# A fused four-layer network: where the windowed attention's first projections and its late score stacks stand in the order of work

## The chip, the cores and the metric

The kernel runs on one NeuronCore of one Trainium2 chip, as one program. The core has five engines with an instruction queue each, and they meet only through semaphores: TensorE (PE, matmuls from SBUF into the eight banks of PSUM, with its weight loads shown apart as PEld), VectorE (DVE), ScalarE (ACT, which works functions such as Exp and Gelu from tables that it has to load), GpSimd (POOL) and SyncE (SP, which here issues most DMA transfers). The metric is the time of one execution on the device in microseconds; less is better.

## What is computed

The input x holds 8 sequences of 256 tokens with 128 features each. Twelve sub-layers are added to it in turn: half a feed-forward layer, a mixer, half a feed-forward layer, in each of four macaron layers, every one of them behind a layer normalisation without parameters. The changed code is in the third macaron layer:

```python
x = x + 0.5 * _L2_ffn_ref(_layernorm(x, axis=-1), ...)      # 16 experts, top 4
x = x + _L2_attn_ref(_layernorm(x, axis=-1), ...)           # linear and windowed attention
x = x + 0.5 * _L2_ffn_ref(_layernorm(x, axis=-1), ...)      # the same 16 experts again

def _L2_attn_ref(x, ...):
    h = _layernorm(x, ln_g, ln_b)
    lin_out = _linear_attention(h @ wq_lin + bq_lin, h @ wk_lin + bk_lin, h @ wv_lin + bv_lin)
    win_out = _window_attention(h @ wq_loc + bq_loc, h @ wk_loc + bk_loc, h @ wv_loc + bv_loc, rel_bias)
    gate_in = jnp.concatenate([lin_out, win_out, h], axis=-1)
    gate = jax.nn.sigmoid(jnp.maximum(gate_in @ wg1 + bg1, 0.0) @ wg2 + bg2)
    out = gate * lin_out + (1.0 - gate) * win_out
    return out @ wo + bo + x
```

The linear attention takes elu(q) + 1 and elu(k) + 1, sums k times v over a sequence and divides by a sum of q times k. The windowed attention has 16 heads of 8 features; each token looks at the 65 tokens within 32 of it, with a learned bias for each distance, and a softmax. The experts compute gelu(x w1 + b1) w2 + b2 with 128 features and 256 hidden units for all 16 experts, weighted by the routing (zero for twelve of the sixteen). The layers before are a sign-weighted feed-forward layer, full softmax attention, a top-2 expert layer and four Mamba layers; those behind are a low-rank quantised feed-forward layer and another attention.

## The kernel before

**Stages.** The stream x stays in SBUF for the whole program, transposed, as xT (128 features by 2048 tokens). `tile_macaron` runs a list of stages: Attn0, Moe1, Mamba, Moe1, Moe2, Attn2, Moe2, Attn3. Expert stages work on four chunks of 512 tokens (CH), attention stages on eight sequences of 256 (SEQ). A stage has `open` (its pools, loads, constants), `steps` or `prepare` (a generator of what must be done before a chunk or sequence can be worked on: normalisation, projections), `main` (the work itself, also a generator), `enter` (what is made once the stage before has ended) and `run`. A stage's pools lie on the other side of SBUF from those of the stage before.

**The wished order.** Everything is issued by generators that are woven together. `weave` (L314) steps through the main generator and, after its step i, draws steps of the generator `ahead` as long as `at * MAIN < i * prep`, where `at` counts the steps drawn. `joined` and `early` take two generators in turns, the second for n steps at most; `mix` shares turns by size. So class constants say what is prepared beside what: MAIN is the number of main's steps, PREP the number of steps of the next stage's generator to be drawn beside the last chunk of the stage before, and EARLY two numbers of steps to be drawn beside the second and the third chunk. Where they are not set, EARLY is (0, 0). `Moe.run` (L530) opens the next stage at its second chunk and passes it those steps at the second, third and fourth chunk. `Attn2.run` uses Attn2's PREP too, in its own loop over sequences: beside the main work of sequence s it draws the steps of `mix(stack(s + 1), project(s + 2))`, which has 29 of them.

**The real order.** The Tile framework then schedules these instructions again with a simulated timeline, so the order of each engine's queue is not the source's; a build's listing of each engine's instructions tells it.

**The experts (Moe2).** `main` works each of 16 experts in two halves of 128 hidden units: matmuls into a bank `h`, the Gelu on ScalarE (32 a chunk, 128 in all), a multiplication by the routing weight on VectorE, a split into a rounded high part `yh` (ScalarE) and the rest `yl` (GpSimd), and matmuls into the bank `o`. The routing weights come as `c<-rows` transfers that SP issues; three such tiles are kept in turn. At a chunk's end VectorE adds `o` to xT.

**Attn2, for each sequence.** The diff touches this class.

- `project` (L1821): the two normalisations (ln_c is the centred tile, pp a bank for a projection, `rsqrt` takes a power on GpSimd), h; then q and k of the windowed attention, each as a rounded part `hi` and the rest `lo`, written to DRAM (`scr`, three writes for each); then the linear attention: `em` (an exponential), `ql`, `kv`, `ek` (an exponential), `kvs`, `den`, `lin`. Ten steps.
- `stack` (L1903): brings `scr` back into the stacked tiles of one of three sets; four heads share the 128 partitions, 32 for each, of which 24 hold hi, hi and lo, and two more hold the row maxima on the side of q and ones on the side of k. Then the row maxima: in two halves (the first and the second maxima), eight times a matmul of qs and ks with a matmul that adds the band of biases, into a bank `mx`, and a maximum on VectorE (`nm`, L1946). A transposition brings the 16 maxima of a half into rows, ScalarE and VectorE round them into `nh` and `nl`, and SP issues four transfers that put them into qs (L1957), so that the scores come out of the matmuls with the maximum already subtracted. 19 steps.
- `main` (L2011): eight tiles of scores (`sp`), VectorE adds the band (`pr`), ScalarE takes the exponential in place, and matmuls by vs and by ones sum into the bank `acc`; then the division, the gate and the output projection (`tail`). MAIN is 11, its number of steps.

**The sets.** `stacks` (L1782) makes a set: qs (128 x 4 x 256), ks (128 x 4 x 4 x 256), vs. Each ks[:, e] holds the keys of one head in four and must be zero in the partitions of the others, so the whole set is filled with zeros first and later only partly written. The fills are copies of a broadcast zero: qs on VectorE (L1791), ks for e = 0 and 2 on VectorE (L1797) and for e = 1 and 3 on ScalarE (through `m.act`, whose instructions all have line L175), each of 128 x 1024; four DMAs write the ones (L1798), and GpSimd clears vs (L1802). Sequences use the sets in the order 0, 1, 2, 0, 1, 2, 1, 0 (SETS). Set 0 is made in `open`, at the experts' second chunk. Sets 1 and 2 are made in `enter`, behind the experts' last chunk, in the pool "a2s", since they lie where the experts' tiles were. Set 0 is given up only with the whole stage. In the trace the experts' matmuls, bias additions and so on have the line of the helper that issued them: L142 for matmuls, L151 for `tt`, L175 for `act`, L171 for the loading of a table in front of an activation, L209 for yl.

Of the kernel before, what the change touches and what calls it, by code (L numbers as in the profile page):

```python
# [255 lines left out]
class Stage:  # L256
# [3 lines left out]
    EARLY = (0, 0)  # L260
# [27 lines left out]
    def enter(self):  # L288
        pass
# [109 lines left out]
class Moe(Stage):  # L399
# [130 lines left out]
    def run(self, st, then):  # L530
        ready, after = list(st), None
        for c in range(NCH):
            if c == NCH - 3:
                with self.m.behind():
                    after, gen = then()
                splits, left = after and after.splits(), after and len(after.todo)
            st = ready.pop(0)
            if c == NCH - 1:
                n = after.PREP if after else 0
                if left:  # L540
                    gen, n = self.early(gen, splits, left), n + left
                return self.weave(self.main(c, st), (after, gen), n)
            to, rest, n = c + self.DEPTH, self.m.rest, 0
            own = self.steps(to) if to < NCH else iter(())
            parts = [rest] if rest else []
            if c >= NCH - 3 and left:

                parts.append((splits, len(after.todo) // 3))
                left -= len(after.todo) // 3
            if c >= NCH - 3 and after:  # L550

                parts.append((gen, after.EARLY[c - NCH + 3]))
            for part in parts:
                own, k = self.joined(own, *part)
                n += k
            st = self.weave(self.main(c, st), (self, own), (self.PREP if to < NCH else 0) + n)
            if to < NCH:
                ready.append(st)
            if rest:
                self.m.rest = self.m.under.close()  # L560


class Moe1(Moe):


    MAIN, PREP, EARLY = 9, 7, (1, 8)
# [85 lines left out]
class Moe2(Moe):  # L652


    MAIN, PREP, EARLY = 16, 16, (1, 3)
# [218 lines left out]
class Attn0(Stage):  # L874


    MAIN, PREP = 17, 12
# [315 lines left out]
class Mamba(Stage):  # L1193


    MAIN, PREP, EARLY = 16, 44, (2, 16)
# [539 lines left out]
class Attn2(Stage):  # L1736


    MAIN, PREP = 11, 30

    SETS = (0, 1, 2, 0, 1, 2, 1, 0)

# [39 lines left out]
    def stacks(self, pool, i):  # L1782

        nc = self.nc
        qs = self.t(pool, [P, 4, SEQ], f"qs{i}", dtype=F32R)
        ks = self.t(pool, [P, 4, 4, SEQ], f"ks{i}", dtype=F32R)
        vs = self.t(pool, [P, 2, 4, 160], f"vs{i}")
        none = self.one[:, 8:9].to_broadcast([P, 4 * SEQ])  # L1790
        nc.vector.tensor_copy(qs[:].rearrange("p m t -> p (m t)"), none)  # L1791
        for e in range(4):
            dst = ks[:, e].rearrange("p m t -> p (m t)")
            if e % 2:
                self.m.act(dst, none, AF.Copy)
            else:
                nc.vector.tensor_copy(dst, none)  # L1797
            nc.sync.dma_start(  # L1798
                ks[32 * e + 24 : 32 * e + 26, e].bitcast(F32),
                self.ones[:].unsqueeze(1).to_broadcast([2, 4, SEQ]),  # L1800
            )
        nc.gpsimd.memset(vs[:], 0.0)  # L1802
        return qs, ks, vs
# [173 lines left out]
    def enter(self):  # L1977
        self.ps = self.pool("a2p", 2, late=True, space=PSUM)
        self.mk = self.pool("a2m", 2, late=True)
        self.more = ExitStack()  # L1980
        tp = self.m.tc.tile_pool(name="a2s", bufs=1, side=self.side, reuse_waits="tile")
        sk = self.more.enter_context(tp)
        self.sets += [self.stacks(sk, 1), self.stacks(sk, 2)]

    def run(self, st, then):
        ready, half = st
        for s in range(NB - 2):
            ahead = self, self.mix(self.stack(s + 1, half), self.project(s + 2))
            ready, half = self.weave(self.main(s, ready), ahead)
        after, gen = then(False)  # L1990
        n = after.EARLY[1] if after else 0
        main = self.main(NB - 2, ready)
        st = self.weave(main, (self, self.early(self.stack(NB - 1, half), gen, n)), 19 + n)
        self.more.close()
        rest = []

        def main():
            rest.append((yield from self.main(NB - 1, st)))

        if after:  # L2000
            after.load()
        res = self.weave(main(), (after, gen), after and after.PIECES)
        if after is None:
            self.finish(rest[0])
        else:

            m = self.m
            m.rest, m.under, self.sb = (rest[0], 4), self.sb, ExitStack()
        return res
# [84 lines left out]
class Attn3(Stage):  # L2094


    MAIN, PREP, EARLY = 5, 10, (4, 9)
# [130 lines left out]
    def project(self, s):  # L2228
# [54 lines left out]
        with m.tc.issue_after(moved.ins):  # L2283
            for i, st in enumerate(stacks):
                for e in range(2):

                    for n, k in enumerate((0, 0, 1) if i else (1, 0, 0)):
                        at = 64 * e + 16 * n
                        nc.sync.dma_start(
                            st[at : at + 16, :, :].rearrange("d (h b) t -> d h (b t)", b=2).bitcast(F32),  # L2290
                            scrs[i][k].rearrange("(h e d) t -> e d h t", e=2, d=16)[e],
                        )
        yield
        return *stacks, vs, hs

    def values(self, hs):
# [301 lines left out]
```

## Time and profile before

The time is 2558.17 us, the median of three executions (2551.15 to 2559.72). The profile was taken of one more execution:

| | us |
|---|---|
| the profiled execution | 2557.26 |
| its span, first to last instruction | 2555.5 |
| PE busy, 11655 matmuls | 2302.1 (90%) |
| VectorE busy | 1938.1 (76%) |
| ScalarE busy | 1879.4 (74%) |
| GpSimd busy | 1608.0 (63%) |
| PE's mean granted clock | 0.954 of full speed |
| bytes moved by DMA | 271.65 MB, 106 GB/s |

The stages around the change, from the windows of the trace (busy us of each engine, and PE's granted clock):

| stage | from to | length | PE | VectorE | ScalarE | GpSimd | clock |
|---|---|---|---|---|---|---|---|
| Moe2, first | 1490 to 1742 | 252 | 239.1 | 198.0 | 200.1 | 151.3 | 0.99 |
| Attn2 | 1742 to 1957 | 215 | 189.2 | 167.4 | 111.8 | 30.8 | 0.97 |
| Moe2, second | 1957 to 2200 | 243 | 226.0 | 178.9 | 187.1 | 126.6 | 0.98 |

The limits of the stages are those that the trace of xT's updates shows, to about a microsecond, and work of neighbouring stages overlaps there. A row of windows gives, behind the limits, the length, then for each of PE, weight loads, VectorE, ScalarE and GpSimd the busy us with the number of instructions in brackets, then PE's granted clock, the DMA engines' busy share and GB/s. A row of the chain of waits has the start, the length and the engine with tile and line; "x2" stands for two instructions running on, "issue" for time in which the engine waited for nothing that the profile shows.

### The profile page before, as it was taken

Reading aid. Unit: us, or ns where it says so; the run is one execution under the profiler, and the core shown is the slowest. Engines: PE = TensorE matmul, PEld = TensorE weight load, DVE = VectorE, ACT = ScalarE, POOL = GpSimd, SP = SyncE. Lnnn points to the kernel's source line nnn. Section 1 sums busy time; section 2 is a strip of 40 time slices with the busy share of each in tenths; the row PEclk is TensorE's granted clock in tenths of the full one; section 3 lists DMA queues with packets and bytes.
Section 4 is the critical chain, followed back from the end, with each engine's and each line's share of the span. In section 5 each row is a group of like instructions: output and inputs, shape, how many; then the busy total and the mean of one; then the engine's idle time right before and its main releaser. Section 6 shows DMA issues by size and latency. Waiting matters only on the chain. (4 is left out here: it accounts for less than half of the span.)

```text
span 2555.5 us, 36909 instructions
## 1 busy us (share of the span) xinstructions
PE 2302.1 (90%) x11655; PEld 1429.0 (56%) x11655; DVE 1938.1 (76%) x3150; ACT 1879.4 (74%) x4373; POOL 1608.0 (63%) x1194
## 2 busy tenths in 40 slices
PE   6999999988988898988897899998998999799997
PEld 5776776843333333333322577776776777566665
DVE  3655666558999999999999788867877877477664
ACT  5877877797777777777764578785555788799885
POOL 2657555559899999999988676552112555554432
PEclk8999999999899999999988899999999999999998
DMA  6676656233444433344432593321225324234420
GB/s 163 173 191 187 159 122 178 75 93 75 104 102 104 111 78 82 84 120 101 93 75 58 151 285 121 110 87 46 71 56 180 114 75 116 41 64 70 79 46 9
DMA packets 138275, 271.65 MB, mean 106 GB/s; under 512 B 19328, under 2 KB 43456, under 8 KB 137696
## 3 DMA queue, kind: packets, MB, share of 16 engines
q1 hardware_dynamic: 136576, 265.56, 40.6%
q10 hardware_dynamic: 1248, 3.48, 0.6%
q8 instruction: 93, 1.52, 0.3%
q14 instruction: 102, 0.84, 0.1%
q0 software_dynamic: 256, 0.25, 0.0%
HBM read 151.54 MB, written 33.16 MB: 72 GB/s over the span
## 5 line engine op out<-in xcount | busy, mean ns | idle before, releaser
L1528 POOL TENSOR_TENSOR hs<-hs,cl 128x1024 f32<-128x1024 f32 x256 | 602.3, 2371 | 68.0 <-DVE hs L1522 43.3
L1522 DVE TENSOR_TENSOR_SCAN hs<-dA,up 128x1024 f32<-128x1024 f32 x192 | 439.1, 2287 | 23.8 <-DVE up L151 0.9
L142 PE MATMUL y<-hs,ysel 128*64 128x512 f32 x1024 | 305.6, 679 | 30.6 <-POOL hs L1528 26.8
L1162 POOL TENSOR_SCALAR pr<-pr,sums 128x256 f32<-128x256 f32 x192 | 175.9, 925 | 166.1 <-DVE sums L1157 149.8
L175 ACT ACTIVATE dA<-dt,negA 128x510 f32<-128x510 f32 x384 | 252.0, 715 | 0.2
L151 DVE TENSOR_TENSOR up<-up,du 128x1024 f32<-128x1024 f32 x192 | 233.3, 1215 | 20.4 <-PE up L142 14.9
L175 ACT ACTIVATE h<-h,vec 128x512 f32<-128x512 f32 x256 | 168.4, 667 | 54.1 <-PE h L142 50.9
L142 PE MATMUL pp<-xp,w 128*128 128x512 f32 x480 | 173.7, 482 | 26.9 <-ACT pre L175 26.2
L235 POOL TENSOR_TENSOR ln_r<-ln_r,mhalf 128x2 f32<-128x2 f32 (+2 forms) x116 | 90.4, 781 | 168.5 <-ACT ln_r L175 166.3
L142 PEld LDWEIGHTS pp<-xp,w 128*128 128x128 f32 x480 | 90.3, 201 | 126.8 <-ACT pre L175 61.7
L1482 POOL TENSOR_TENSOR hs<-du,bl 128x1024 f32<-128x1024 f32 x64 | 151.6, 2369 | 1.8 <-DVE pre L151 1.8
L1522 DVE TENSOR_TENSOR_SCAN hs<-up,hs 128x1024 f32<-128x1024 f32 x64 | 145.0, 2265 | 0.2 <-ACT up L175 0.2
L209 POOL TENSOR_TENSOR yl<-y,yh 128x512 fp32r<-128x512 f32 x64 | 83.0, 1297 | 96.7 <-ACT yh L175 93.2
L175 ACT ACTIVATE pr<-sp,nmax 128x256 f32<-128x256 f32 x256 | 121.7, 487 | 26.1 <-DVE nmax L1149 7.1
L142 PE MATMUL up<-bp,bsel 128*128 128x512 f32 x192 | 101.6, 530 | 41.6 <-DVE hs L1522 38.6
L142 PEld LDWEIGHTS y<-hs,ysel 128*64 128x64 f32 x1024 | 54.1, 144 | 144.3 <-issue 76.5
L175 ACT ACTIVATE ln_q<-pp 128x128 f32<-128x128 f32 x348 | 98.9, 284 | 38.0 <-PE pp L142 33.7
L209 POOL TENSOR_TENSOR yl<-z,yh 128x512 fp32r<-128x512 f32 x72 | 92.2, 1292 | 51.6 <-ACT yh L175 44.0
L1149 DVE TENSOR_REDUCE nmax<-sp 128x2 f32<-128x512 f32 x128 | 87.5, 687 | 48.7 <-PE sp L142 47.8
L151 DVE TENSOR_TENSOR h<-h,c 128x512 f32<-128x512 f32 x128 | 89.1, 696 | 36.9 <-ACT h L175 29.5
L142 PE MATMUL h<-hh,wh 128*128 128x512 f32 x256 | 104.9, 410 | 9.5 <-DVE y L151 7.5
L175 ACT ACTIVATE ln_c<-pp,ln_r 128x128 f32<-128x128 f32 x332 | 99.5, 375 | 16.7 <-POOL ln_r L235 16.0
(444 smaller groups left out, 6836.6 us busy)
## 6 DMA issues: line engine op xcount, KB each, us to landing
c<-rows SPq DMA_DIRECT2D x64, 512.0 KB
cl<-states SPq DMA_DIRECT2D x62, 512.0 KB
c<-rows SPq DMA_DIRECT2D x64, 256.0 KB
dt<-dt SPq DMA_DIRECT2D x128, 128.0 KB
du<-du SPq DMA_DIRECT2D x128, 128.0 KB
k<-kh SPq DMA_DIRECT2D x60, 256.0 KB
kl<-kl SPq DMA_DIRECT2D x60, 256.0 KB
st<-scr SPq DMA_DIRECT2D x96, 128.0 KB
```

Of the source, the lines that this page charges most:

```text
L142: return self.pin(self.nc.tensor.matmul(out, lhsT, rhs, start=start, stop=stop))
L151: return self.pin(self.nc.vector.tensor_tensor(out, in0, in1, op))
L175: i = self.nc.scalar.activation(out, in_, func, **kw)
L209: i = (lower or self.nc.vector).tensor_tensor(lo, x, hi, ALU.subtract)
L235: self.nc.gpsimd.tensor_tensor(out, out, self.mhalf[:, 0 : out.shape[-1]], ALU.pow)
L1149: nc.vector.tensor_reduce(nmax[:], sp[:], AX.X, ALU.max, negate=True)
L1162: self.turned = nc.gpsimd.tensor_scalar(pr[:, t, :], pr[:, t, :], sums[:, t : t + 1], None, ALU.mult)
L1482: self.m.pin(self.nc.gpsimd.tensor_tensor(self.hs[g][:], du[:], b, ALU.mult))
L1522: m.pin(nc.vector.tensor_tensor_scan(x[:].rearrange("p g t -> p (g t)"), self.decays.pop(g).rearrange("p g b t -> p (g b t)"), u[:].rearra ...
L1528: m.pin(nc.gpsimd.tensor_tensor(x[:], x[:], c, ALU.mult))
```

## The change

Three things, all in Attn2.

1. The steps of its generator that are drawn beside the experts: none at the second chunk, 10 at the third and 20 at the fourth, in place of none, none and 30. As PREP is used in the stage's own loop too, there 20 of 29 steps are wished beside the main work of a sequence, and the other nine behind it.
2. The four ks fills of sets 1 and 2 all go to ScalarE, in place of two of each set. Set 0's stay shared between VectorE and ScalarE.
3. `enter` makes only set 1; `run` makes set 2 behind the main work of sequence 0 (in the source), before the steps of sequence 2, the first that uses it, are drawn.

```diff
 class Attn2(Stage):
-    MAIN, PREP = 11, 30
+    MAIN, PREP, EARLY = 11, 20, (0, 10)
...
         for e in range(4):
             dst = ks[:, e].rearrange("p m t -> p (m t)")
-            if e % 2:
+            if e % 2 or i:
                 self.m.act(dst, none, AF.Copy)
             else:
                 nc.vector.tensor_copy(dst, none)
...
         tp = self.m.tc.tile_pool(name="a2s", bufs=1, side=self.side, reuse_waits="tile")
-        sk = self.more.enter_context(tp)
-        self.sets += [self.stacks(sk, 1), self.stacks(sk, 2)]
+        self.sk = self.more.enter_context(tp)
+        self.sets.append(self.stacks(self.sk, 1))

     def run(self, st, then):
         ready, half = st
         for s in range(NB - 2):
             ahead = self, self.mix(self.stack(s + 1, half), self.project(s + 2))
             ready, half = self.weave(self.main(s, ready), ahead)
+            if s == 0:
+                self.sets.append(self.stacks(self.sk, 2))
```

## The prediction

> **What bounds the kernel now.** I read the busy table by slices first, to see which engine is full around the edited stage, then PE's busy time by windows, then the chain of waits across the hand-over, then single engines in order of time. The edit touches 1587 to 1833 us: the first 16-expert stage's last three chunks, and the first two sequences of the linear and window attention behind it. The x updates of VectorE at 1586.9, 1639.1, 1686.0 and 1741.9 us end the experts' four chunks. The third and fourth, by windows (length, then busy us and instructions of PE, weight loads, VectorE, ScalarE, GpSimd, then PE's granted clock, DMA):
>
> ```profile
> 1639.10:1686.00 46.90, 46.77 (x203) 38.03 (x204) 34.22 (x56) 34.99 (x61) 25.64 (x25) 1.00 0.37 115
> 1686.00:1741.90 55.90, 52.25 (x234) 39.79 (x233) 38.29 (x78) 47.70 (x84) 28.92 (x34) 1.00 0.19 62
> ```
>
> PE is full in the third chunk and loses 3.6 us in the fourth, nearly all of it where ScalarE changes its function table. Then the hand-over, by the same columns:
>
> ```profile
> 1741.70:1748.30 6.60, 1.91 (x9) 1.18 (x8) 6.36 (x10) 3.90 (x4) 2.81 (x2) 0.89 0.03 7
> 1748.30:1752.00 3.70, 3.60 (x13) 3.12 (x14) 2.76 (x6) 0.00 (x0) 0.00 (x0) 0.50 0.05 11
> 1752.00:1757.30 5.30, 2.81 (x11) 1.73 (x9) 1.49 (x7) 2.50 (x11) 1.40 (x2) 0.82 0.17 50
> 1757.30:1761.60 4.30, 4.25 (x17) 3.62 (x17) 1.84 (x4) 2.31 (x5) 0.00 (x0) 0.63 0.54 138
> ```
>
> PE stands idle for 7.3 us of these 20 and runs much of the rest at half its clock. The chain of waits (start, us, what) says why:
>
> ```profile
> 1742.63 0.81 DVE qs L1791
> 1743.44 2.25 DVE ks L1797 x2
> 1745.69 0.40 DVE nm L1946
> 1746.09 0.60 DVE qs L1791
> 1746.69 1.20 DVE ks L1797 x2
> 1747.89 0.41 DVE nm L1946
> ...
> 1748.35 1.98 PE pp L142 x6
> ...
> 1754.85 0.44 SPq L1957
> 1755.28 0.04 issue
> 1755.33 1.78 DMA qs<-nl
> 1757.11 0.25 issue
> 1757.35 1.19 PE sp L142 x4
> ```
>
> VectorE's six fills of sets 1 and 2 stand between the row maxima (nm) of sequence 0, which hold PE's three free banks; these fills cost 4.86 us of the path. Only when the last maxima have gone by DMA into qs may the scores (sp) start, 15.4 us behind the experts' last matmul.
>
> **EARLY and PREP: sequence 0 sooner.** Ten steps of the generator are drawn in the third chunk and 20 in the fourth instead of 30 in the fourth, so as before some ten are left to the hand-over in the source. The scheduler reorders them, so I go by the order listing of both builds, counting the experts' 128 Gelus. Sequence 0's em exponential moves from behind Gelu 102 to 74, its ek from 104 to 78, its lin from 110 to 84; sequence 1's hi from 118 to 93, its em from 118 to 112, ek from 122 to 118. Its normalisation, hi, lo and scr writes were in the third chunk already. Five of the eight second maxima, both matmuls of sequence 1's centring and the transposition of the maxima now stand ahead of the experts' last two matmuls: eight pairs of a set and band matmul at 0.30 us from start to start, 2.4, centring, transposition and two ln_c 0.6, so 3.0 us of PE work goes in front of the experts' end. As PE is full there, that end moves back 3.0 us; it is moved, not added.
>
> ScalarE pays in the third chunk. Its 35.0 us of 46.9 get two exponentials (0.42), four table loads (1.28 each), three copies (1.0) and sequence 1's normalisation, h and hi (4.8): 11.8 together, so 46.8, just as much as PE has. The rows for one exponential:
>
> ```profile
> 1686.23 1.28 ACT L171 ACT_TABLE_LOAD   x1
> 1687.52 0.42 ACT L175 ACTIVATE em<-em 128x256 f32<-128x256 f32 x1
> 1687.96 1.28 ACT L171 ACT_TABLE_LOAD   x1
> ```
>
> Each excursion withholds 3.0 us from the Gelus. PE has four h banks to ride it out: the two of sequence 0 cost PE 1.3 us of idle now, the two of sequence 1 (held open for 8.4 us) 1.9. Least: all four as cheap as the first two, 2.5 us. Most: fully exposed, 12. With the third chunk's ScalarE full but the fourth's down to 36 of about 53 us, I take 4.4 against 3.9 us now (0.5 worse; ends -1.4 and +8).
>
> The row shows the load ending 0.01 us before the exponential. The Trainium skill, page "ScalarE: Activation LUTs", section "What ACT_TABLE_LOAD costs", adds a 1.38 us drain to the same 1.28 us load and so speaks against this move; no drain stands in these rows. By it the four loads of the third chunk would take 10.6 us instead of 5.1, which would put ScalarE 5.5 us over.
>
> SP issues the same 14 scr transfers (0.36 to 0.6 us each) ahead of other c<-rows loads. Of those three are kept in turn, and SP waits for their buffers, not they for SP (28.4 us for six issues behind 1656.8); cost nothing under that cover, 0.4 to 0.9 us a transfer without. On GpSimd one of sequence 1's powers (0.71) now stands before the last yl (1.28): up to 0.7 at the experts' end, inside the 4.4. PREP also paces the attention's own six sequences (20 of their 29 steps instead of all): I cost this at nothing, because the listing has the same PE order in both builds from sequence 1's second maxima to the last sequence. Without that, nine steps with the 4.7 us from maxima to scores would come bare six times, 28 us.
>
> **Fills: four from VectorE to ScalarE, set 2 later in the source.** No fill may start before the experts' last matmul (ScalarE's now start at 1741.70, released by PE o). VectorE loses four (3.45 us on the chain) and keeps two qs (0.81 and 0.60), which now stand behind all the maxima. ScalarE has eight instead of four. The row:
>
> ```profile
> 1741.70 3.90 ACT L175 ACTIVATE ks<-one 128x1024 fp32r<-128x1024 f32 x4 [1.68 <-PE o L142]
> ```
>
> In the listing both sets' fills stand before the first pr exponential, so "a sequence later" is not what the queue does. From the experts' last matmul, T': set 1 until 3.9, two ln_c 0.6, set 2 until 8.4, first exponential 0.7, first acc at T' + 9.2. Behind those fills wait all pr exponentials and, through them, all acc matmuls. GpSimd's two memsets (2.81) run beside it.
>
> PE in the meantime: from the transposition of the maxima to the first scores took 5.4 us (1751.91 to 1757.35: nh, nl, four issues on SP, 1.78 us of DMA). The transposition now stands about 1.4 us before T', so scores start at T' + 4.0; five tiles of them, paced by VectorE's 0.80 a tile, and 0.9 us of others end near T' + 8.5. Then set 1's own DMAs: behind the maxima's issues (T' + 1.8) SP has eight of ones and zeros at 0.7, eight of scr at 0.41, then 3.0 us to landing (as at 1885.01): set 1's first maxima at T' + 13.2.
>
> **The sum.** Before, set 1's first maxima start 18.9 us behind the experts' end with 6.2 us of matmuls at full clock between: 12.7 lost (7.3 idle, the rest half clock). After, 13.2 with 6.2 (five tiles of scores and two of acc in place of the maxima): 7.0 lost, 5.7 better. Then set 1's second maxima wait for nl by DMA with 1.9 us of other matmuls to cover it instead of 5.1: 3.8 lost to 2.3, 1.5 worse. 5.7 - 1.5 - 0.5 = 3.7 us. The profiled span of 2555.5 lies in a run of 2557.26, 0.9 below the median of 2558.17: I expect 2554.4. With the exponentials' loss at its least, 2.5 us, it is 2552.5, with all 12 us of it 2562. The second experts and the last attention are shuffled a little in the listing; 43 us of PE idle lie there in 555, and I allow 3 either way. Three runs lay 8.6 us apart.
>
> As to the clock, the row has 0.50 from 1748.3 to 1752 behind 4.8 us of idle in 6.6. The Trainium skill ("TensorE: Matmul & The Clock Gate", "Part 1: The HAM clock gate") says that one idle window of about 3.4 us halves the clock until as long a busy one. By that the 4.0 us hole left at T' would be followed by scores at half rate, 3 us of them costing 1.5 more; as they end before ScalarE does, the sum would stay.
>
> **Rivals.**
> ScalarE becomes the bound of the third chunk (slower, 0.24): for it, 46.8 us against 46.8 and a queue kept in order; against, PE lost only 1.3 us at two excursions. It decides once more than 8.1 us of the 12 are exposed; at 12, 2562.
> The hole closes further (faster, 0.20): ScalarE waits on nothing in the fourth chunk and all table loads cost 2.5, and the second maxima's DMA stays covered (1.5): 2554.4 - 1.9 - 1.5 = 2551; with the late shuffle at its good end 2548. For it: 12.7 us are lost there; against, eight fills in a row.
> The change does not do what it says (0.08): the reordering scheduler had half of sequence 0's projections in the third chunk already; gain and loss cancel, 2558.
> My forecast has 0.48.
>
> **The numbers.** About 0.3%, 7.7 us, is what a measurement here can tell from no change: faster is below 2550.5, slower above 2565.8. Faster: half of the second rival and 0.12 of the forecast's lower tail, 0.22. Slower: 0.10 of the first, 0.06 for what the late shuffle may add, 0.16. The range: 2554.4 less 5 and the shuffle's 3, 2546; 2562 and 2 of the 3, 2564. The forecast's own is 2550 to 2559.
>
> **What would show it.** Right: ScalarE near 47 us in the third chunk; eight ks fills back to back, ending 8.4 us behind the experts' last matmul with pr right behind; first maxima on set 1 near 13 us behind it; no L1797 on VectorE but set 0's; the loop at 26 us a sequence as before. Wrong: PE idle before h matmuls at the exponentials of the third chunk beyond 4 us, a loop longer than that, or a hand-over as long as 19 us.

## The result, and the profile after

The changed kernel takes 2563.61 us (median of 10 executions, 2559.82 to 2570.26) against 2558.11 us of the kernel before (10 executions, 2551.15 to 2566.96): a ratio of 1.0028, with an interval of 1.0014 to 1.0041. A second comparison, 12 executions against 35, gave 1.0004 (0.9987 to 1.0021). So the change costs between nothing and some 7 us where 3.7 us of gain were forecast; the time lies in the stated range (2546 to 2564), but on the other side of the time before from the forecast. The profiled execution took 2564.42 us, with a span of 2562.6.

The third and fourth chunk of the experts, by windows (length, then busy us and instructions of PE, weight loads, VectorE, ScalarE, GpSimd, then PE's granted clock, DMA share, GB/s):

```profile
1642.40:1698.40 56.00, 54.25 (x249) 43.88 (x248) 41.63 (x76) 45.32 (x82) 28.96 (x31) 1.00 0.35 111
1698.40:1752.30 53.90, 49.00 (x209) 37.34 (x207) 37.59 (x67) 39.41 (x70) 26.18 (x28) 0.97 0.15 50
```

The third chunk has grown from 46.9 to 56.0 us, the fourth has shrunk from 55.9 to 53.9. ScalarE is busy for 45.3 of the third's 56.0 us and is not its bound. PE does more there (249 matmuls instead of 203) and is idle for 1.75 us instead of 0.1, in the fourth for 4.9 instead of 3.65. Then ScalarE's queue in order of time (start, length, line, what):

```profile
1752.11 3.89 ACT L175 ACTIVATE ks<-one 128x1024 fp32r<-128x1024 f32 x4
1755.91 0.60 ACT L175 ACTIVATE ln_c<-pp,rs 128x128 f32<-128x128 f32 x2
1756.41 3.89 ACT L175 ACTIVATE ks<-one 128x1024 fp32r<-128x1024 f32 x4
1760.20 1.36 ACT L175 ACTIVATE pr<-pr 128x640 f32<-128x640 f32 x2
```

That is the queue as it was forecast: both sets, one behind the other, and the first score exponential 8.1 us behind the start of the fills (forecast 8.4). The chain of waits across the hand-over (start, us, what):

```profile
1751.58 0.51 PE o L142
1752.09 0.02 issue
1752.11 1.11 ACT ks L175 x2
...
1754.02 1.99 ACT ks L175 x2
1756.01 0.51 ACT ln_c L175 x2
1756.51 0.96 ACT ks L175
1757.47 0.29 SPq L1798
...
1760.54 0.42 SPq L1916
...
1762.26 3.16 DMA ks<-scr
1765.41 0.83 issue
1766.25 1.03 PE mx L142 x4
```

No VectorE fill stands on it any more. Fills, SP's issues and the transfer of the keys follow each other, and set 1's first maxima (mx) start 13.9 us behind the end of the experts' last matmul (1752.31), forecast 13.2, before 18.9.

So where did the loss come from? The x updates of VectorE cut the span into stages that the kernels share. The table counts from the start of the last x update of the Moe1 stage (1530.18 us in the profile of before), to which the expectations below refer as the first chunk's end; "x of sequence 1" is the update that ends the edited attention for sequence 1. (Moe2 begins there, not at 1490 us as the table of stages had it.) Two profiles stand for each of three programs; the fills alone are the third and tenth run below.

| us from there to | before | changed | fills alone |
|---|---|---|---|
| the experts' end | 211.8, 211.9 | 219.4, 219.7 | 211.8, 212.0 |
| x of sequence 1 | 291.6, 293.1 | 292.4, 294.3 | 290.6, 292.2 |
| x of sequence 3 | 344.3, 344.8 | 344.1, 346.0 | 342.3, 343.9 |
| the second experts' end | 658.4, 663.1 | 659.2, 662.2 | 655.4, 657.7 |
| the end | 1022.7, 1025.3 | 1026.5, 1031.2 | 1014.1, 1015.6 |
| length of the last attention | 364.3, 362.2 | 367.2, 369.0 | 358.7, 358.0 |

By means, the changed kernel is 0.5 us late at sequence 3, on time (-0.1) at the end of the second experts, and 4.9 late at the end of the program. The edited stage came out even, and the loss lies in the last attention (with the feed-forward layers woven into it), some 440 us behind the edit. No line of it was touched: the scheduler put its instructions in another order. (Between two profiles of one program this table differs by up to 4.7 us, so its single rows are rough; the experiments below say how far the order can be told from chance.)

### The profile page after: what moved, and what is told of

It is laid out like the page before. It is cut to its first block, busy times and chain, and to the rows that moved or that the text cites. A ratio compares the mean times of both kernels' runs of the same rounds, so it can differ in the third digit from the quotient of the medians.

```text
span 2562.6 us, 36926 instructions
## 1 busy us (share of the span) xinstructions
PE 2313.9 (90%) x11655; PEld 1437.7 (56%) x11655; DVE 1936.6 (76%) x3146; ACT 1883.3 (73%) x4377; POOL 1607.4 (63%) x1194
## 5 line engine op out<-in xcount | busy, mean ns | idle before, releaser
L142 PE MATMUL up<-bp,bsel 128*128 128x512 f32 x192 | 100.8, 526 | 37.8 <-DVE hs L1522 35.3
L142 PE MATMUL h<-hh,wh 128*128 128x512 f32 x256 | 104.5, 408 | 11.4 <-DVE y L151 7.7
```

The lines of the kernel that those rows point to most:

```text
L142: return self.pin(self.nc.tensor.matmul(out, lhsT, rhs, start=start, stop=stop))
```

## The experiments

The profiles compare stages, the ratios whole runs. Each variant is built from the kernel before (b) or the changed one (a). The listing tells which order PE has in the last attention: B is that of the kernel before, A that of the changed one, F that of the third run, L that of the fourth. These letters are not those of the theories A to D in the expectations. The traces show the same four orders: within one letter all 2,055 matmuls behind the second experts stand in one order (run 2 departs from B by 14).

**One part at a time.** Runs 1 and 2: the early steps alone, and with set 2 made later.

```diff
 b, run 1
-    MAIN, PREP = 11, 30
+    MAIN, PREP, EARLY = 11, 20, (0, 10)
 run 2: the same, and set 2 made behind s == 0 as in the change
```

> The kernel before with the first part alone: MAIN, PREP, EARLY = 11, 20, (0, 10). PE's order in the last attention is that of the kernel before, word for word. Theory A (the edited region gains about what it loses, and the 5.5 us of the whole change lie in the new order of the last attention): 2558 +- 3, region from the first chunk's end to the x update of sequence 2 at 318.6 +- 2 us as before. Theory B (the steps drawn early stall PE beside the experts, and that is the loss): 2561 to 2564, with the third and fourth chunk some 7 us longer and at most 4 us won back behind them. Theory C (the fills in a row on ScalarE are the loss): 2553 to 2556, since here VectorE's six fills no longer stand between the second maxima.

> The first and the third part: steps drawn early, set 2 made a sequence later, its fills and set 1's shared between VectorE and ScalarE as before. PE's order behind the second sequence is that of the kernel before but for some 30 rows. Theory A: 2555 to 2559. Theory B: 2561 to 2564, like the first run. Theory C: 2550 to 2555, as neither engine has more than three fills of a set in a row.

Ratios 1.0003 (0.9984 to 1.0021) and 1.0004 (0.9987 to 1.0021), with medians of 2564.60 and 2561.27 us where the kernel before took 2560.79 in the same comparison. The experts' end is at 219.4 and 217.8, 7.6 and 6.0 us late, and given back by sequence 3 (342.9 and 343.6). The last attention takes 361.8 and 364.7 us, with order B. Theory C, which expected a gain of the first run, is out. The experts' end is late as theory B says, but nothing of it is left at sequence 3, where theory B had at most 4 us won back.

Runs 3 and 4: the fills alone, and the fills with set 2 later.

```diff
 b, run 3
-            if e % 2:
+            if e % 2 or i:
 run 4: the same, and set 2 made behind s == 0 as in the change
```

> The second part alone: all eight ks fills of sets 1 and 2 on ScalarE, steps drawn as before. The last attention's order differs from both kernels' in some 1000 rows. Theory A: the hand-over gains about 3.4 us (four fills of 0.6 to 1.1 us leave VectorE's queue between the maxima), and the total is anything from 2552 to 2562, by the order of the last attention alone. Theory B: 2554 to 2556. Theory C: the first score exponential waits for eight fills; hand-over as long as before or longer, 2560 to 2564.

> The second and third part: the change without the steps drawn early. Theory A: hand-over 3 us shorter, total 2552 to 2562 by the last attention's order. Theory B: 2553 to 2556, the gain of the fills without the experts' stalls. Theory C: 2560 to 2564.

Ratios 0.9974 (0.9956 to 0.9991) and 0.9998 (0.9982 to 1.0014). With the fills alone the kernel is faster: 2553.77 us against 2560.79. At sequence 3 both are 2.0 us ahead of the first profile of before (342.3, 342.2; but the third run's kernel came to 343.9 in its second profile), and the last attention takes 358.7 us with order F and 365.3 with order L. Theory C expected the third run to be slower than before, and theory B 2553 to 2556 us of the fourth, which took 2560.73.

**The same region with another end.** The listing of a build tells its order before it runs, and small edits around the hand-over leave the last attention in one of a few orders. So regions and ends can be paired. Run 5 is the changed kernel again; the others:

```diff
 a, run 6: set 2's qs fill on GpSimd                          (end B)
-        nc.vector.tensor_copy(qs[:].rearrange("p m t -> p (m t)"), none)
+        (nc.gpsimd if i == 2 else nc.vector).tensor_copy(qs[:].rearrange("p m t -> p (m t)"), none)
 a, run 7                                                     (end F)
-    MAIN, PREP, EARLY = 11, 20, (0, 10)
+    MAIN, PREP, EARLY = 11, 20, (0, 9)
 run 3's kernel, run 8                                        (end A)
-    MAIN, PREP = 11, 30
+    MAIN, PREP, EARLY = 11, 29, (0, 1)
```

> The changed kernel once more, beside its variants. Theory A (the order that the scheduler gives the second experts and the last attention is the loss): ratio 1.002 to 1.003, from the first chunk's end of the first experts to the x update of sequence 3 within 1 us of before, the last attention 366 to 368 us against 362 to 364 of the kernel before and of the first run, which have one order there. Theory D (the edited stage is the loss, the last attention is noise): ratio the same, the last attention 362 to 365.

> The changed kernel, with set 2's qs fill on GpSimd instead of VectorE. PE's order around the hand-over differs from the changed kernel's in 78 rows; in the last attention it is word for word that of the kernel before. Theory A: the loss is gone, ratio 0.999 to 1.001, the last attention 362 to 365 us. Theory D: as the changed kernel, 1.002 to 1.003.

> The changed kernel with EARLY (0, 9) instead of (0, 10). Around the hand-over its order is close to the changed kernel's; in the last attention it is word for word that of the third run (the fills alone), which was the fastest there, 358.7 us. Theory A: ratio 0.997 to 0.999, the last attention 358 to 360. Theory D: 1.001 to 1.003.

> All eight fills on ScalarE, both sets at the hand-over, one step drawn in the third chunk and 29 in the fourth. The hand-over is near the third run's; behind it, from the third sequence to the end, the order is the changed kernel's but for 7 rows, in the last attention word for word. Theory A: the last attention 366 to 368 us and the ratio 1.000 to 1.003, though the hand-over gains as in the third run. Theory D: 0.996 to 0.998 like the third run.

| run | end | x of sequence 3 | last attention | ratio |
|---|---|---|---|---|
| 5, changed again | A | 346.0 | 369.0 | 1.0004 (0.9987 to 1.0021) |
| 6 | B | 351.0 | 362.2 | 1.0006 (0.9990 to 1.0022) |
| 7 | F | 346.0 | 356.9 | 0.9980 (0.9965 to 0.9996) |
| 8 | A | 344.5 | 364.9 | 1.0000 (0.9985 to 1.0015) |

Run 5's ratio misses what both theories expected (1.002 to 1.003), and its x of sequence 3 lies 1.2 to 1.7 us behind the profiles of before where theory A allowed 1; its last attention is long, as theory A says (369.0, expected 366 to 368), and outside theory D's 362 to 365. Run 7 is the clearest: the changed kernel with one step less in the third chunk has the same x of sequence 3 (346.0) and a last attention that is 10 to 12 us shorter. In run 6 the last attention came back to 362.2, as theory A says, but its hand-over got 5 to 7 us longer, PE waiting 2.9 us for set 1's keys and 2.5 for its maxima, so its total doesn't test theory A by itself. Run 8's ratio lies at the edge of what theory A expected, and its last attention is 1.1 us shorter than the 366 to 368 us expected.

**Repeats, and the table loads.** Runs 9 and 10 are the kernel before and run 3's once more. Runs 11 (changed) and 12 (before) have

```diff
-        m.act(em[:], em[:], AF.Exp)
+        m.act(em[:], em[:], AF.Exp if s > 1 else AF.Tanh)
 and the same for ek
```

> The kernel before once more, for the spread between two executions of one program, stage by stage. Ratio 1.000. If the last attention's order is what counts, that stage lies at 362 to 365 us again (364.3, 361.8, 364.7 and 362.2 in the four profiles with this order so far); if those differences are chance, anywhere from 357 to 369.

> The third run's kernel once more (all ks fills of sets 1 and 2 on ScalarE, nothing else). Theory A: last attention 357 to 360 us, ratio 0.996 to 0.999. If the third run was chance: ratio 0.999 to 1.001.

> The changed kernel, with sequence 0's and 1's em and ek computed by Tanh (from the table in which Gelu is) instead of Exp, so that no table is loaded beside the experts. If the table loads hold up the experts, the last chunk's end, +7.6 us in the changed kernel, comes down to +5 (the matmuls moved in front of it); if not, it stays at +7 to +8. In the last attention it has the order of the third run: 357 to 360 us by theory A.

> The kernel before with the same edit: sequence 0's and 1's em and ek by Tanh. The last chunk's end comes 2 to 4 us earlier if the table loads cost what PE stood idle around them (1.3 and 1.9 us); not at all if other work takes their place. The last attention has the order of before: 362 to 365 us.

Run 9: ratio 1.0005 (0.9991 to 1.0020), last attention 362.2. Run 10: 0.9977 (0.9962 to 0.9992), 358.0; the third run was no chance. Run 11: 0.9995 (0.9982 to 1.0009); experts' end at 216.0 instead of 219.6, x of sequence 1 at 291.8 instead of 293.4, last attention 357.8, end F; yet the ratio is not that of the other runs with F, for its profile is at the end of the second experts at 665.5 us, 4.7 later than the profiles of before (mean 660.7). Run 12: 0.9991 (0.9975 to 1.0008); the experts' end came later, not earlier (214.5), since the scheduler now moved more work in front of it; x of sequence 1 at 290.2 instead of 292.4, last attention 366.0, 1 us above what was expected of order B. At x of sequence 1 the table loads thus cost 1.6 us in the changed kernel and 2.2 in the one before. Each figure is from one profile, two profiles of one program differ there by 1.5 and 1.9 us, and both edits also changed which matmuls stand ahead of the experts' end; so no difference between the kernels is shown there.

**Edit and order the other way round.**

```diff
 b, run 13: both late qs fills on GpSimd, ks shared as before  (end F)
-        nc.vector.tensor_copy(qs[:].rearrange("p m t -> p (m t)"), none)
+        (nc.gpsimd if i else nc.vector).tensor_copy(qs[:].rearrange("p m t -> p (m t)"), none)
 run 3's kernel, run 14                                        (end B)
-    MAIN, PREP = 11, 30
+    MAIN, PREP, EARLY = 11, 28, (0, 2)
```

> The kernel before with nothing but the qs fills of sets 1 and 2 moved from VectorE to GpSimd; the ks fills stay shared. PE's order is word for word that of the third run (all ks fills on ScalarE), from the first to the last matmul. If the third run is faster by its order in the last attention, this one is too: last attention 357 to 360 us, ratio 0.996 to 0.999. If it is faster because ScalarE fills, this one is 0.999 to 1.001.

> All ks fills of sets 1 and 2 on ScalarE as in the third run, with two steps drawn in the third chunk and 28 in the fourth; PE's order in the last attention is that of the kernel before. If the order there decides: last attention 362 to 366 us, ratio 0.999 to 1.001. If the fills on ScalarE are the gain: 0.996 to 0.998.

Run 13: 0.9983 (0.9969 to 0.9996), last attention 356.9. Run 14: 1.0004 (0.9989 to 1.0018), 361.8. In run 13 all 11,655 matmuls of the trace stand in the third run's order, and run 14 has the third run's fills with order B. The time goes with the order, not with the engine that fills. Whether ScalarE's fills bring something of their own (0.9974 and 0.9977 against 0.9983) stays open; the intervals overlap.

Over all profiles the last attention takes 361.8 to 366.0 us with order B (seven executions, mean 363.3), 364.9 to 369.0 with A (three, 367.1), 356.9 to 358.7 with F (five, 357.7). The four kernels with F (one of them twice) have quite different hand-overs, and none comes up to the lowest B. A's lowest lies inside B's range. The stages ahead of it shift too: the second experts by 3.3 us between two profiles of the kernel before (212.0 and 215.3 us from the last sequence's x to their end), and over all profiles their end lies at 655.4 to 671.3 us (before: 658.4 and 663.1). That is as wide as the spread of the last attention, and their part is not told from chance. So the order sets the length of the last attention, but a whole kernel's ratio only follows it on average: 0.9974 to 0.9995 with F, 0.9991 to 1.0006 with B, 1.0000 to 1.0028 with A.

**What the orders do.** The whole last attention by windows, in the kernel before, the changed kernel and the third run:

```profile
2188.62:2552.89 364.27, 330.67 (x2057) 221.10 (x2055) 219.64 (x547) 300.10 (x844) 154.34 (x140) 0.96 0.29 54
2192.81:2560.05 367.24, 331.76 (x2057) 223.17 (x2055) 218.37 (x547) 299.60 (x844) 154.47 (x140) 0.95 0.27 54
2185.62:2544.34 358.72, 328.80 (x2057) 222.11 (x2055) 221.82 (x547) 297.65 (x844) 153.90 (x140) 0.96 0.29 55
```

The third and fourth sequence of it, in the kernel before:

```profile
2333.70:2370.03 36.33, 34.97 (x235) 23.66 (x235) 25.26 (x66) 32.46 (x86) 17.35 (x16) 1.00 0.38 73
2370.03:2411.26 41.23, 39.72 (x258) 26.95 (x258) 26.37 (x68) 36.73 (x104) 19.70 (x18) 1.00 0.37 68
```

in the changed kernel, with a stretch of 6.2 us at the end of the third:

```profile
2333.41:2373.43 40.02, 36.47 (x227) 24.56 (x229) 23.51 (x64) 32.45 (x89) 17.37 (x15) 0.93 0.35 66
2373.43:2415.95 42.52, 39.80 (x260) 26.08 (x260) 27.56 (x70) 35.05 (x92) 17.65 (x16) 0.99 0.31 66
2367.20:2373.40 6.20, 5.83 (x16) 3.48 (x17) 1.21 (x3) 2.00 (x6) 1.24 (x2) 0.52 0.13 47
```

and in the third run:

```profile
2329.00:2368.39 39.39, 38.95 (x256) 26.68 (x254) 29.50 (x71) 35.62 (x98) 21.32 (x19) 1.00 0.43 91
2368.39:2404.91 36.52, 35.63 (x243) 24.82 (x242) 27.74 (x70) 33.47 (x92) 17.48 (x16) 1.00 0.44 80
```

PE's idle time (length less busy) is 1.4 and 1.5 us with B, 3.6 and 2.7 with A, 0.4 and 0.9 with F. Over the whole last attention it is 33.6 us before, 35.5 after, 29.9 in the third run. With A there are two new holes; the first on PE's queue (in brackets the idle time and what ended it):

```profile
2363.91 0.50 PE L142 MATMUL sp<-st,st 48*128 48x256 f32 x4
2365.82 0.50 PE L142 MATMUL sp<-fs,spread 128*128 128x256 f32 x2 [1.41 <-DVE at L2418]
2366.55 0.51 PE L142 MATMUL sp<-fs,spread 128*128 128x256 f32 x2 [0.22 <-ACT at L175]
```

The matmul that PE has next waits for VectorE (`at`); the second hole, of 1.49 us, is the same one sequence later. And behind the first the clock is at 0.52 for 6.2 us.

These two sequences are not the whole account, though. The attention's own x updates cut the last attention into stretches (means, in brackets the range; us):

| order | to the first update | the next four | the rest |
|---|---|---|---|
| B (seven) | 102.0 (101.3 to 103.1) | 159.9 (159.8 to 160.0) | 101.5 (100.5 to 103.4) |
| A (three) | 101.8 (101.1 to 103.2) | 161.3 (158.8 to 163.4) | 103.9 (103.0 to 104.5) |
| F (five) | 99.0 (98.2 to 100.3) | 158.4 (158.3 to 158.4) | 100.4 (100.1 to 100.8) |

Within the next four, A wins 3.1 us on B in the second sequence (39.4 against 42.5). At full clock (run 8) its four take 158.8 us, less than B's, holes and all; what A loses there comes with the lowered clock behind the holes (161.8 and 163.4 us), and another 2.4 us lie in the rest. F gains most, 3.0 us, ahead of the first update. What makes those two outer stretches longer or shorter was not traced.

## Why the prediction was wrong, point by point

**Fills.** Right in kind and nearly in size: the fills of both sets one behind the other, the exponentials behind them, set 1's first maxima at 13.9 instead of 13.2 us, first scores 1.6 us behind the end of the experts' last matmul instead of 4.0. From the experts' end to the x of sequence 1 the kernel became 6.7 us shorter (80.5 to 73.8, means), where 4.2 of gain and 3.0 moved, 7.2 together, were forecast.

**EARLY and PREP.** The first step that failed, by its size: the prediction put 3.0 us of PE's work in front of the experts' end and charged 0.5 us of waiting for the exponentials, 3.5 together; that end moves back 7.7 us. All eight pairs of second maxima run ahead of the experts' last matmuls (the text counted five, the sum eight), and with the rest of what was drawn early 23 more matmuls and 4.8 us of PE's busy time come before that end (203.0 to 207.8 us from the table's start), not 3.0; PE's idle time grows by 2.9 us, not 0.5. The matmuls are moved, not added, but the waiting behind the end fell by only 6.7 - 4.8 = 1.9 us instead of 4.2. So the forecast 3.7 us of gain is 1.0 us of loss at sequence 1 and 0.5 at sequence 3, within the spread of two profiles of one program. The rival that ScalarE becomes the bound of the third chunk did not happen (45.3 busy of 56.0 us). But the waits around the exponentials grew: between the x updates that end the second and the fourth chunk PE is idle for 7.3 us after and 3.8 before, where the forecast had 4.4 and 3.9. Without the table loads it is 3.7 (run 11) and 2.3 (run 12), so the loads go with some 3.6 us of it after and 1.6 before, one profile each and with other matmuls moved too. At x of sequence 1 the difference no longer shows.

**The late shuffle.** The second step that failed. The prediction said that "the second experts and the last attention are shuffled a little in the listing" and allowed 3 us either way. Of the 2,055 matmuls that the trace of either kernel has behind the second experts at most 1,525 keep their order among each other, the other engines' queues are shuffled with them (395 of VectorE's 547 instructions keep theirs), and that is worth +3.8 us (A against B, whose ranges overlap) to -5.6 us (F against B); at sequence 3 all runs but the sixth lie within 3.6 us of the kernel before. By the profiles the sign came from a place that the forecast treated as noise; by whole runs order A stands at 1.0000 to 1.0028 and B at 0.9991 to 1.0006, so how much of the loss it makes up stays open. In the edited stage alone, gain and loss cancel as in the third rival, but not for the reason that it gave: the work did move, and 7.7 us lost ahead of the experts' end stand against 6.7 won behind it.

**The loop.** Right: no stall at 20 steps instead of 29; from x of sequence 1 to that of sequence 3 it is 51.7 us after and 52.2 before.

**What the clock did.** At the hand-over PE ran at half clock for 6.8 us (0.50 from 1753.05 to 1759.87) while the exponentials waited for ScalarE's fills anyway, as the prediction had it, and for 3.4 us more (from 1766.70) behind the 2.3 us that it waited for set 1's keys, which the prediction did not have. That a hole of 1.41 us in the last attention is followed by 0.52, and not in every execution, was not foreseen; it goes with the spread of order A from 364.9 to 369.0 (last section).

## What to carry to other kernels

Where a scheduler orders the program, an edit's effect does not end where the edit ends: list the order of every stage behind it, and treat a stage whose order changed as changed. The expected few microseconds of a hand-over are no more than such a reshuffle brings, so a part is judged stage by stage, in several builds with different orders behind it, before its total is credited to it. The version to keep here is the fills on ScalarE alone, with its order F: 0.9974 and 0.9977 in two comparisons, faster than both kernels; but the gain belongs to this build and may go with the next edit.

## What the runs showed of the hardware

The same hole in one program has different prices. Both profiles of the changed kernel and the eighth run's have the two holes of about 1.4 and 1.5 us. Behind the first one and the second one, in the second profile of the changed kernel:

```profile
2372.80:2379.00 6.20, 5.58 (x17) 3.57 (x18) 2.61 (x3) 3.40 (x12) 2.63 (x3) 0.72 0.23 85
2415.20:2421.40 6.20, 6.20 (x25) 3.19 (x25) 2.66 (x4) 3.54 (x13) 2.02 (x4) 0.60 0.23 85
```

and behind the first one in the eighth run's:

```profile
2366.00:2380.00 14.00, 13.40 (x81) 8.32 (x82) 6.32 (x11) 8.31 (x21) 3.44 (x4) 1.00 0.37 90
```

By windows whose limits are set to its fall and rise, the clock is at 0.50 for 6.8 us behind the first hole in the first profile, for 3.4 and 6.8 us behind the two in the second, and at 1.00 behind the other three. Against the eighth run (37.55 and 42.07 us) the third and fourth sequence took 2.5 and 0.5 us longer in the first profile (40.02 and 42.52) and 1.6 and 3.0 in the second (39.13 and 45.11). So a hole of 1.4 or 1.5 us halved the clock for 3.4 or 6.8 us or not at all. The Trainium skill ("TensorE: Matmul & The Clock Gate", "Part 1: The HAM clock gate") says that activity is judged in windows that run freely, which agrees with a price that changes from execution to execution; but it names an idle window of some 3.4 us as what throttles, and here PE was still busy for 1.77, 2.09 and 1.92 us of the 3.41 us before the three falls of the clock.

With the same order and the clock at 1.00, a stretch's time reproduces to a few hundredths of a microsecond: the third and fourth sequence of the last attention took 39.39 and 36.52 us in the third run, and 39.38 and 36.53 in the thirteenth, another kernel with the same order. What differs most between executions of this stage is the clock, and the stretch ahead of its first x update (101.3 to 103.1 us with order B), for which no cause was looked for.
